# Attention and a convolutional layer on one core: fourteen of sixteen partial sums sent by transfers, four more half groups multiplied in parts

## The chip, the cores and the metric

The kernel runs on one core of one Trainium2 chip. Its time is the device time in microseconds (us). Where several runs of a kernel are shown, the median stands for them. A core has five engines that the text speaks of by short names: PE (TensorE, the matrix engine; PEld is its loading of weights), DVE (VectorE), ACT (ScalarE), POOL (GpSimd) and SP (SyncE, which here only issues transfers).

## The reference

Two layers are computed one after the other on a tensor of 4 images of 64 x 64 pixels with 256 channels. The first is self-attention over all 4096 pixels of an image. The second is a small convolutional network with a 3 x 3 local attention behind it.

```python
# layer 0, for each image: N = 4096 tokens, C = 256
q, k, v = x @ Wq + bq, x @ Wk + bk, x @ Wv + bv        # q, k: 32 channels; v: 256
attn  = softmax(q @ k.T)                               # 4096 x 4096
x     = gamma * (attn @ v) + x
# layer 1
p     = depthwise_conv3x3(x, w_perc)                   # 256 -> 768 channels
hid   = gelu(w_up1 @ p)                                # 768 -> 512
h     = x + w_up2 @ hid                                # 512 -> 256
ql, kl, vl = split(h @ w_qkv.T)                        # 256 each
w     = softmax over the 9 neighbours of (ql . kl[neighbour]) / 16
out   = h + sum over the 9 neighbours of w * vl[neighbour]
```

All tensors are in fp32.

## The kernel before

**Slots and points.** The four images are cut into 8 blocks of 512 queries each, so there are 32 slots. The kernel handles one slot after the other, and inside a slot it walks over the 4096 keys in 16 steps, called points. A point deals with one half group, which is two key tiles of 128 keys; half groups are numbered n = 0 to 15, and n = 2G + half. For a half group, PE computes the energies (`energy`, L404), ACT takes their exponentials into a tile `p` of 128 x 1024 numbers (L409), and PE multiplies the exponentials by the values into `acc` (`product`, L435, L446, L458). Energies and exponentials run two points ahead of the product that uses them: at point i the kernel issues the energy of half group i + 2, makes the pieces of half group i + 1, and issues the product of half group i.

**Three kinds of product.** A plain fp32 half group is two tiles of fp32 matmuls (L435). A half group "in parts" replaces each fp32 matmul by three cheaper fp32r matmuls. For it the exponentials are split into a high part (`ph`, made on ACT at L414), a low part (`pl`, on DVE at L502) and a gap (`pg`, on DVE at L506), and the values into matching pieces that lie in DRAM (`packed_h`, `packed_f`) and are loaded as `v` and `vf`. Half groups 2, 4, ..., 14 are in parts (`IN_PARTS`). In half groups 3, 5, ..., 13 only the second of the two tiles is in parts (`ONE_IN_PARTS`); its pieces are `oh` (ACT, L420), `ol` and `og` (DVE, L486 and L489) and the loaded `vo` (from `packed_o`). Half groups 0, 1 and 15 are plain. This holds in the 25 slots that `full(s)` names, which are slots 3 to 6, 8 to 14, 16 to 22 and 24 to 30; the remaining slots use fewer pieces.

**The softmax denominator.** It is the sum of all exponentials of a slot. Eleven of the half groups of a full slot (3, 5, 7, 9, 11, 13 and 4, 6, 8, 10, 12) are summed by transfers: POOL issues a DMA that adds `p` into one of two tiles `sent` (`send`, L476 and L478). The others (0, 1, 2, 14 and 15) are added into `den` by DVE in `add_up` (L504). At the slot's end DVE adds the two `sent` tiles to `den` (L513), folds its halves together (L514), and reduces them to `parts` (L532, L533). PE multiplies those by a fixed matrix (`dps`, L551), DVE takes the reciprocal (L554), and `on_all` spreads it over the tile by a copy (L540, DVE) and a transpose (L543). Two ACT instructions (L561) and DVE instructions (L567 to L575) then finish the block.

**What else lies in a slot.** Layer 1 runs behind attention, cut into jobs, one list entry for each point: `hidden_part` (`hid` matmuls, L779, with DVE additions at L786 and an ACT copy of `hid_a` at L792), `local_product`, `update`, `guide`, `local_values` (`lv`, L999), `scores`, `local_sum` (POOL, L1088) and `border`. At `update`, `border_terms` computes the products of border pixels on DVE, as pairs of L971 and L972: two pairs in most slots, and four in those that touch the upper or lower edge of an image. The depthwise convolution, called perceive, is 54 steps of DVE work in each slot: taps (L666) and additions of tiles (L672). A list named `share` says how many of the 54 are issued at each point, behind the point's `add_up`.

**Order.** Each engine executes its instructions in the order in which the program issues them; the order above is written out by hand in the loop over slots and points. Tiles come from pools of a fixed number of buffers. Those that matter here are `p` (3 buffers), `vs` (4 buffers, for `vo`, `oh`, `ol`, `og` and the pieces of values in the projections), `hid` (1), `xc` (2) and `sent` (1). A tile of a pool that is full waits until the oldest one is no longer used. The core of one point of the loop is:

```python
if one_in_parts(slot, point + 1): load_one(slot, point + 1)    # SP: vo
...                                                            # SP: keys, values
if in_parts(*behind): high_part(*behind)                       # ACT: ph
if one_in_parts(slot, point + 1): high_one(slot, point + 1)    # ACT: oh
if after[0] < NSLOT: energy(*after, half)                      # PE, ACT
if by_dma(slot, point + 1): send(slot, point + 1)              # POOL
...                                                            # SP: vf
for do in jobs[point]: do()                                    # layer 1
product(slot, G, half)                                         # PE
add_up(slot, *divmod(point + 1, 2))      # DVE: ol, og, pl, den, pg
... # perceive, up to sum(share[: point + 1]) steps            # DVE
```

At the first and the last point there are exceptions, which the functions below show. Between images (the last slot of each image but the fourth) the projections of the next image are issued too; `project_v` makes the pieces of the values and writes them to DRAM.

## Time and profile before

| what | value |
|---|---|
| median of three runs | 3248.18 us (3248.05 to 3251.35) |
| the profiled execution's own time | 3249.86 us |
| its span in the trace | 3248.1 us |
| granted TensorE clock, mean | 0.999 |
| POOL's transfers into `sent` | 287 of 512 KB, median 6.2 us from issue to landing |
| SP's loads of `vo` | 150 of 256 KB, median 4.1 us |
| DMA traffic | 616.58 MB, 190 GB/s on average |
| share of 16 DMA engines | 40.5% for SP's queue, 24.8% for POOL's |
| chain of waits, by engine | PE 75%, DVE 17%, issue 3%, DMA 2%, ACT 1%, POOL 1% |

The span is what the hardware profiler recorded from the first to the last instruction of one execution, and that execution's own time is 1.8 us longer. A busy share is the time in which an engine had an instruction under way, divided by the span. Line numbers such as L502 are lines of the kernel before. A name such as `pl` in a row of the profile stands for all tiles of that name.

### The profile page before, as it was taken

Reading aid. Unit: us, or ns where it says so; the run is one execution under the profiler, and the core shown is the slowest. Engines: PE = TensorE matmul, PEld = TensorE weight load, DVE = VectorE, ACT = ScalarE, POOL = GpSimd, SP = SyncE. Lnnn points to the kernel's source line nnn. Section 1 sums busy time; section 2 is a strip of 40 time slices with the busy share of each in tenths; the row PEclk is TensorE's granted clock in tenths of the full one; section 3 lists DMA queues with packets and bytes.
Section 4 is the critical chain, followed back from the end, with each engine's and each line's share of the span. In section 5 each row is a group of like instructions: output and inputs, shape, how many; then the busy total and the mean of one; then the engine's idle time right before and its main releaser. Section 6 shows DMA issues by size and latency. Waiting matters only on the chain.

```text
span 3248.1 us, 37927 instructions
## 1 busy us (share of the span) xinstructions
PE 3218.2 (99%) x12286; PEld 2223.2 (68%) x12286; DVE 2866.3 (88%) x4380; ACT 1449.8 (45%) x1845; POOL 724.1 (22%) x970
## 2 busy tenths in 40 slices
PE   9999999999999999999999999999999999999998
PEld 5557767766776677676767767776677677667655
DVE  4779899898999999988999999998799999999895
ACT  4434444444444444444444444444444444444331
POOL 3201122221222221222122222211221122222021
PEclk9999999999999999999999999999999999999999
DMA  7767766777667777667766677776777666777100
GB/s 254 222 165 202 194 187 191 202 230 205 196 187 200 211 211 191 186 196 243 205 191 193 184 200 213 208 194 192 253 210 195 190 191 185 201 210 204 49 25 28
DMA packets 289964, 616.58 MB, mean 190 GB/s; under 512 B 97424, under 2 KB 98464, under 8 KB 289632
## 3 DMA queue, kind: packets, MB, share of 16 engines
q1 hardware_dynamic: 228608, 409.47, 40.5%
q0 software_dynamic: 53472, 191.17, 24.8%
q10 hardware_dynamic: 7680, 13.44, 1.1%
q8 instruction: 102, 1.67, 0.2%
q14 instruction: 102, 0.84, 0.1%
HBM read 386.24 MB, written 76.41 MB: 142 GB/s over the span
## 4 chain that ended last, share of the span: by engine, by line
PE 75%; DVE 17%; issue 3%; DMA 2%; ACT 1%; POOL 1%; SPq 0%; ACTq 0%; DVEq 0%; POOLq 0%
PE acc L435 19%; PE acc L458 11%; PE dx L836 5%; PE e L404 5%; DVE perc L666 5%; PE hid_bc L779 5%; PE hid_de L779 4%; PE hid_gf L779 4%; PE acc L446 4%; PE v L339 3%; PE lv L999 3%; PE g L932 3%; PE lo L1133 2%; PE hid_a L779 2%; DVE den L513 2%
## 5 line engine op out<-in xcount | busy, mean ns | idle before, releaser
L666 DVE SCALAR_TENSOR_TENSOR perc<-xp,wb,perc 128x526 f32<-128x526 f32 (+1 forms) x1356 | 941.2, 758 | 1.5 <-ACT perc L662 1.4
L435 PE MATMUL acc<-p,v 128*128 128x512 f32 x1872 | 854.5, 592 | 0.2 <-ACT v L355 0.2
L409 ACT ACTIVATE p<-e 128x1024 f32<-128x1024 f32 x512 | 524.3, 1024 | 546.6 <-PE e L404 490.5
L435 PEld LDWEIGHTS acc<-p,v 128*128 128x128 f32 x1872 | 351.7, 190 | 341.9 <-issue 328.2
L478 POOL DMA_DIRECT2D sent<-p x235 | 201.3, 857 | 1125.6 <-ACT p L409 948.9
L404 PE MATMUL e<-qa,ka 128*128 128x512 f32 x1024 | 368.3, 440 | 2.0 <-ACT p L409 1.1
L414 ACT ACTIVATE ph<-p 128x1024 fp32r<-128x1024 f32 x203 | 214.3, 1056 | 213.2 <-PE acc L458 131.6
L506 DVE SCALAR_TENSOR_TENSOR pg<-pl,ph 128x1024 fp32r<-128x1024 f32 x203 | 267.2, 1316 | 9.0 <-PE e L404 0.5
L502 DVE TENSOR_TENSOR pl<-p,ph 128x1024 fp32r<-128x1024 f32 x203 | 252.2, 1242 | 18.5 <-ACT ph L414 16.8
L458 PE MATMUL acc<-ph,v 128*128 128x512 f32 x812 | 264.0, 447 | 0.2 <-DMA v<-packed_h 0.2
L404 PEld LDWEIGHTS e<-qa,ka 128*128 128x128 f32 x1024 | 189.5, 189 | 88.2 <-issue 45.7
L420 ACT ACTIVATE oh<-p 128x512 fp32r<-128x512 f32 x150 | 94.5, 630 | 317.6 <-PE acc L446 265.4
L836 PE MATMUL dx<-hid,wup 128*128 128x512 f32 x512 | 229.8, 592 | 0.0
L458 PE MATMUL acc<-pl,vf 128*128 128x512 f32 x812 | 223.3, 397 | 0.0
L458 PE MATMUL acc<-pg,vf 128*128 128x512 f32 x812 | 218.7, 391 | 0.9 <-DVE pg L506 0.9
L504 DVE TENSOR_TENSOR den<-den,p 128x1024 f32<-128x1024 f32 x161 | 207.1, 1287 | 5.7 <-ACT p L409 5.3
L1088 POOL TENSOR_TENSOR lsum<-lsum,lp 128x99 f32<-128x99 f32 (+1 forms) x179 | 208.8, 1173 | 11.7
L458 PEld LDWEIGHTS acc<-ph,v 128*128 128x128 f32 x812 | 148.2, 189 | 51.3 <-issue 26.8
L458 PEld LDWEIGHTS acc<-pl,vf 128*128 128x128 f32 x812 | 152.7, 188 | 37.1
L458 PEld LDWEIGHTS acc<-pg,vf 128*128 128x128 f32 x812 | 152.5, 188 | 37.2 <-DVE pg L506 1.4
L802 ACT ACTIVATE hid<-hid,bup 128x512 f32<-128x512 f32 x120 | 80.2, 715 | 211.0 <-DVE hid L786 211.0
L672 DVE TENSOR_TENSOR perc<-perc 128x262 f32<-128x262 f32 x360 | 167.6, 486 | 6.3
(217 smaller groups left out, 4953.3 us busy)
## 6 DMA issues: line engine op xcount, KB each, us to landing
sent<-p POOLq DMA_DIRECT2D x287, 512.0 KB, 6.2
vf<-packed_f SPq DMA_DIRECT2D x203, 512.0 KB, 5.4
v<-packed_h SPq DMA_DIRECT2D x200, 512.0 KB, 4.4
ka<-packed SPq DMA_DIRECT2D x1016, 64.0 KB, 2.8
vo<-packed_o SPq DMA_DIRECT2D x150, 256.0 KB, 4.1
xp<-in_x SPq DMA_DIRECT2D x30, 528.0 KB, 6.1
packed_f<-vlg POOLq DMA_DIRECT2D x28, 512.0 KB, 4.5
xc<-in_x SPq DMA_DIRECT2D x56, 256.0 KB, 3.9
```

Of the source, the lines that this page charges most:

```text
L404: nc.tensor.matmul(e[:, i, :], lhsT=keys[s, G][:, bass.ts(2 * half + i, P)].bitcast(F32R), rhs=queries[s].bitcast(F32R), start=True, stop= ...
L409: nc.scalar.activation(p, e, AF.Exp)
L414: nc.scalar.activation(high.bitcast(F32R), weights[s, G, half], AF.Identity, scale=BELOW)
L435: nc.tensor.matmul(accs[s][c], lhsT=v[:, i, bass.ts(c, P)], rhs=p[:, i, :], start=(first and i == 0), stop=(last and i == 1),)
L458: nc.tensor.matmul(accs[s][to + c], lhsT=w[:, i, bass.ts(c, P)].bitcast(F32R), rhs=x[:, i, :].bitcast(F32R), start=(to > 0 and n == 0 and ...
L502: nc.vector.tensor_tensor(low.bitcast(F32R), p, high, ALU.subtract)
L504: nc.vector.tensor_tensor(den, before, p, ALU.add)
L506: nc.vector.scalar_tensor_tensor(gap.bitcast(F32R), low, -SPLIT, high, ALU.mult, ALU.add)
L666: nc.vector.scalar_tensor_tensor(acc, win, wt, acc, ALU.mult, ALU.add)
L779: nc.tensor.matmul(ps[:, n * C : (n + 1) * C], lhsT=w(j), rhs=rows_of(mixes[s, j][:, kind, :]), start=(j == 0), stop=(j == MULT - 1),)
L836: nc.tensor.matmul(ps, lhsT=wup2[:, d, bass.ts(c, P)], rhs=hids[s][:, d, :], start=(d == 0), stop=(d == NHC - 1),)
L1088: nc.gpsimd.tensor_tensor(to, to, near_ws[block, half][:, t_, of, :], ALU.add)
```

## The change

Seven things change.

- Half groups 1 and 15 join those of which one tile is in parts.
- In half groups 11 and 13 the first tile is in parts as well, so that both tiles are (`BOTH_IN_PARTS`). The four pieces of the first tile lie in one buffer of the pool `hid`.
- `by_dma` of a full slot now holds for half groups 0 to 13, or 2 to 13 in the first block of an image. So DVE adds up only 14 and 15 (and 0 and 1 there). The first half group to be added is no longer known ahead, and `add_up` keeps it in `firsts` until a second one comes.
- The copy in `on_all` moves from DVE to ACT.
- The first product of each border pair (L971) moves from DVE to ACT.
- The list `share` moves perceive steps to earlier points.
- `project_v` makes and stores the additional pieces of the values, and `packed_o` has a place for two tiles of each half group. `product` is written as one list of matmuls, which lets the second accumulator start at half group 1 and end at 15.

Its core as a diff:

```diff
-ONE_IN_PARTS = (3, 5, 7, 9, 11, 13)
-BY_DMA = (ONE_IN_PARTS, (4, 6, 8, 10, 12))
+ONE_IN_PARTS = (1, 3, 5, 7, 9, 11, 13, 15)
+BOTH_IN_PARTS = (11, 13)
+BY_DMA = (3, 5, 7, 9, 11, 13)
+BY_DMA_IF_FULL = tuple(range(14))
...
+        def alone(s, n):
+            return [i for i, ns in enumerate((BOTH_IN_PARTS, ONE_IN_PARTS)) if full(s) and n in ns]
...
+        def load_alone(s, n):
+            for i in alone(s, n):
+                if i:
+                    f, *rest = [tile_of([P, NB], "vs", f"vo_{s}_{n}", 4)] + [None] * 3
+                else:
+                    four = tile_of([P, NHC, NB], "hid", f"vo_{s}_{n}_0")
+                    f, *rest = (four[:, j] for j in range(NHC))
+                forms[s, n, i], rests[s, n, i] = f, rest
+                nc.sync.dma_start(
+                    out=f.rearrange("p (f c) -> p f c", c=C), in_=packed_o[:, block(s, n // 2), i]
+                )
...
+        def high_alone(s, n):
+            for i in alone(s, n):
+                high = rests[s, n, i][0]
+                if high is None:
+                    high = tile_of([P, NB], "vs", f"oh_{s}_{n}", 4)
+                p = weights[s, n // 2, n % 2][:, i, :]
+                nc.scalar.activation(high.bitcast(F32R), p, AF.Identity, scale=BELOW)
+                highs[s, n, i] = high
...
+        def low_and_gap(s, n):
+            for i in alone(s, n):
...
+                nc.vector.tensor_tensor(low.bitcast(F32R), p, high, ALU.subtract)
+                nc.vector.scalar_tensor_tensor(
+                    gap.bitcast(F32R), low, -SPLIT, high, ALU.mult, ALU.add
+                )
...
         def product(s, G, half):
...
+                apart = alone(s, n)
+                todo += [(v[:, i], 0, p[:, i, :], F32) for i in range(2) if i not in apart]
+                for i in apart:
...
+                    todo += [
+                        (v[:, i], 0, highs[at], F32R), (f[:, :C], 0, lows[at], F32R),
+                        (f[:, C:], CH, gaps[at], F32R),
+                    ]
...
         def by_dma(s, n):
-            if n in BY_DMA[1]:
-                return full(s)
-            return 0 < s < NSLOT - 1 and (s < 2 or s % NBLK < NBLK - 1) and n in BY_DMA[0]
+            if full(s):
+                return n in BY_DMA_IF_FULL and (n > 1 or s % NBLK > 0)
+            return 0 < s < NSLOT - 1 and (s < 2 or s % NBLK < NBLK - 1) and n in BY_DMA
...
         def add_up(s, G, half):
...
-            if G == 0 and half == 0:
-                sums[s] = tile_of([P, 2, NB], "den", f"den_{s}")
-                return
...
             if not by_dma(s, n):
-                nc.vector.tensor_tensor(den, before, p, ALU.add)
+                if s in sums:
+                    nc.vector.tensor_tensor(sums[s], sums[s], p, ALU.add)
+                elif s in firsts:
+                    sums[s] = tile_of([P, 2, NB], "den", f"den_{s}")
+                    nc.vector.tensor_tensor(sums[s], firsts.pop(s), p, ALU.add)
+                else:
+                    firsts[s] = p
...
         def on_all(values, turned, out):
-            nc.vector.tensor_copy(
+            nc.scalar.copy(
                 squares(turned), values.unsqueeze(2).to_broadcast([P, NJ, SQ])
             )
...
             for to, of in border_parts(s):
-                nc.vector.tensor_scalar(edge[:, to], of(0), wc[:, 0:1], None, ALU.mult)
+                nc.scalar.mul(edge[:, to], of(0), wc[:, 0:1])
...
-            share = [1, 5, 8, 6, 5, 2, 7, 4, 6, 3, 4, 2, 1, 0, 0, 0]
+            share = [2, 6, 8, 4, 7, 2, 7, 4, 6, 4, 3, 1, 0, 0, 0, 0]
...
+                load_alone(slot, point + 1)
...
+                high_alone(slot, point + 1)
...
-                if by_dma(slot, point + 1):
-                    send(slot, point + 1)
+                at = behind[0], 2 * behind[1] + behind[2]
+                if by_dma(*at):
+                    send(*at)
```

More of the change, by code (lines that the diff above doesn't have):

```diff
@@ L204, in seen @@
             return watched[:, i : i + 1]
-        queries, keys, values, forms, staged = {}, {}, {}, {}, {}
+        queries, keys, values, forms, rests, staged = {}, {}, {}, {}, {}, {}
         packed = tc.dram_tile([NSLOT // 2, 2, 2, 2, CQK, NB], F32, name="packed")
@@ L214, in unshifted @@
         packed_f = tc.dram_tile([P, NSLOT, 2, 2 * C], F32, name="packed_f")
-        packed_o = tc.dram_tile([P, NSLOT, 2, C], F32, name="packed_o")
+        packed_o = tc.dram_tile([P, NSLOT, 2, 2, C], F32, name="packed_o")
         def in_two_sums(s):
@@ L224, in in_parts @@
             return in_two_sums(s) and 2 * G + half in IN_PARTS
-        def one_in_parts(s, n):
-            return full(s) and n in ONE_IN_PARTS
+        def alone(s, n):
+            return [i for i, ns in enumerate((BOTH_IN_PARTS, ONE_IN_PARTS)) if full(s) and n in ns]
         def load_parts(to, s, which):
@@ L322, in load_forms @@
             )
-        def load_one(s, n):
-            forms[s, n] = tile_of([P, NB], "vs", f"vo_{s}_{n}", 4)
-            nc.sync.dma_start(
-                out=forms[s, n].rearrange("p (f c) -> p f c", c=C),
-                in_=packed_o[:, block(s, n // 2)],
-            )
+        def load_alone(s, n):
[9 more added lines that the diff above has]
+                )
         def fresh(name):
@@ L345, in project_v @@
             n = 2 * (s % NBLK) + pair
-            split, one = n in IN_PARTS, n in ONE_IN_PARTS
+            split, one, both = (n in ns for ns in (IN_PARTS, ONE_IN_PARTS, BOTH_IN_PARTS))
             h = packed_h[:, s, bass.ts(pair, 2 * C)].rearrange("p (t c) -> p t c", c=C)
@@ L359, in project_v @@
                 )
-                if not split:
+                if not split and not both:
                     tiles = slice(0, 1 if one else 2)
                     nc.gpsimd.dma_start(out=h[:, tiles], in_=v[:, tiles])
+            if not split and not one:
+                return
+            high = fresh(f"vh_{s}_{pair}")
             if split:
-                high = fresh(f"vh_{s}_{pair}")
-                both = tile_of([P, 2, NB], "sent", f"vlg_{s}_{pair}")
-                both = both.rearrange("p f (t c) -> p f t c", c=C)
+                lg = tile_of([P, 2, NB], "sent", f"vlg_{s}_{pair}")
+                lg = lg.rearrange("p f (t c) -> p f t c", c=C)
+                low, gap = lg[:, 0], lg[:, 1]
                 to = h, packed_f[:, s].rearrange("p f (t c) -> p f t c", c=C)
-            elif one:
-                high = fresh(f"vh_{s}_{pair}")[:, 0:1]
-                both = fresh(f"vlg_{s}_{pair}").rearrange("p f (t c) -> p f t c", c=C)
-                of = of[:, 1:2]
-                to = h[:, 1:2], packed_o[:, s].rearrange("p f (t c) -> p f t c", c=C)
-            else:
-                return
-            low, gap = both[:, 0], both[:, 1]
+            elif both:
+                lg = tile_of([P, 2, NB], "sent", f"vlg_{s}_{pair}")
+                lg = lg.rearrange("p t (f c) -> p t f c", c=C)
+                low, gap = lg[:, :, 0], lg[:, :, 1]
+                to = h, packed_o[:, s]
+            else:
+                high, of = high[:, 0:1], of[:, 1:2]
+                lg = fresh(f"vlg_{s}_{pair}")
+                low, gap = lg[:, 0:1], lg[:, 1:2]
+                to = h[:, 1:2], packed_o[:, s, 1]
             nc.scalar.copy(low, of)
@@ L380, in project_v @@
             nc.vector.tensor_scalar(low, low, SPLIT, None, ALU.mult)
-            for at, part in zip(to, (high, both)):
+            for at, part in zip(to, (high, lg)):
                 nc.gpsimd.dma_start(out=at, in_=part)
@@ L391, in spread_queries @@
             load_parts(queries[s], s, 0)
-        weights, highs, lows, gaps, sent = {}, {}, {}, {}, {}
+        weights, highs, lows, gaps, sent, firsts, started = {}, {}, {}, {}, {}, {}, {}
         sums, accs, lsums, lrdens = {}, {}, {}, {}
@@ L415, in high_part @@
             highs[s, G, half] = high
-        def high_one(s, n):
-            high = tile_of([P, NB], "vs", f"oh_{s}_{n}", 4)
-            p = weights[s, n // 2, n % 2]
-            nc.scalar.activation(high.bitcast(F32R), p[:, 1, :], AF.Identity, scale=BELOW)
-            highs[s, n] = high
+        def high_alone(s, n):
[6 more added lines that the diff above has]
+                highs[s, n, i] = high
@@ new lines, in low_and_gap @@
+        def low_and_gap(s, n):
+            for i in alone(s, n):
+                high, (_, low, gap) = highs[s, n, i], rests.pop((s, n, i))
+                if low is None:
+                    low, gap = (tile_of([P, NB], "vs", f"o{x}_{s}_{n}", 4) for x in "lg")
+                p = weights[s, n // 2, n % 2][:, i, :]
+                nc.vector.tensor_tensor(low.bitcast(F32R), p, high, ALU.subtract)
+                nc.vector.scalar_tensor_tensor(
+                    gap.bitcast(F32R), low, -SPLIT, high, ALU.mult, ALU.add
+                )
+                lows[s, n, i], gaps[s, n, i] = low, gap
@@ L423, in product @@
         def product(s, G, half):
             p = weights[s, G, half]
-            first = G == 0 and half == 0
-            if first:
-                n = 2 * CH if in_two_sums(s) else CH
-                accs[s] = [bank("acc", f"acc_{s}_{c}") for c in range(n)]
+            n = 2 * G + half
+            if n == 0:
+                accs[s] = [bank("acc", f"acc_{s}_{c}") for c in range(2 * CH if in_two_sums(s) else CH)]
+                started[s] = set()
             v = values[s, G][:, 2 * half : 2 * half + 2]
-            last = G == NG - 1 and half == 1
@@ L431, in product @@
-            if not in_parts(s, G, half):
-                one = one_in_parts(s, 2 * G + half)
-                for i in range(1 if one else 2):
-                    for c in range(CH):
-                        nc.tensor.matmul(
-                            accs[s][c], lhsT=v[:, i, bass.ts(c, P)], rhs=p[:, i, :],
-                            start=(first and i == 0), stop=(last and i == 1),
-                        )
-                if one:
-                    at = s, 2 * G + half
-                    f = forms.pop(at)
-                    for w, to, x in (
-                        (v[:, 1], 0, highs[at]), (f[:, :C], 0, lows[at]), (f[:, C:], CH, gaps[at])
-                    ):
-                        for c in range(CH):
-                            nc.tensor.matmul(
-                                accs[s][to + c], lhsT=w[:, bass.ts(c, P)].bitcast(F32R),
-                                rhs=x.bitcast(F32R), start=False, stop=False,
-                            )
-                return
@@ L451, in product @@
-            f = forms.pop((s, G, half))
-            n = IN_PARTS.index(2 * G + half)
-            for part, (w, to, x) in enumerate((
-                (v, 0, highs[s, G, half]), (f[:, :2], 0, lows[s, G, half]), (f[:, 2:], CH, gaps[s, G, half])
-            )):
-                for i in range(2):
-                    for c in range(CH):
-                        nc.tensor.matmul(
-                            accs[s][to + c], lhsT=w[:, i, bass.ts(c, P)].bitcast(F32R),
-                            rhs=x[:, i, :].bitcast(F32R),
-                            start=(to > 0 and n == 0 and i == 0),
-                            stop=(to > 0 and n == len(IN_PARTS) - 1 and i == 1),
-                        )
+            todo = []
@@ new lines, in product @@
+            if in_parts(s, G, half):
+                f = forms.pop((s, G, half))
+                for w, to, x in (
+                    (v, 0, highs[s, G, half]), (f[:, :2], 0, lows[s, G, half]),
+                    (f[:, 2:], CH, gaps[s, G, half]),
+                ):
+                    todo += [(w[:, i], to, x[:, i, :], F32R) for i in range(2)]
+            else:
+                apart = alone(s, n)
+                todo += [(v[:, i], 0, p[:, i, :], F32) for i in range(2) if i not in apart]
+                for i in apart:
+                    at = s, n, i
+                    f = forms.pop(at)
+                    todo += [
+                        (v[:, i], 0, highs[at], F32R), (f[:, :C], 0, lows[at], F32R),
+                        (f[:, C:], CH, gaps[at], F32R),
+                    ]
@@ new lines, in product @@
+            ends = {0: n == 2 * NG - 1, CH: n == (2 * NG - 1 if full(s) else IN_PARTS[-1])}
+            for k, (w, to, x, kind) in enumerate(todo):
+                last = ends[to] and all(later[1] != to for later in todo[k + 1 :])
+                for c in range(CH):
+                    nc.tensor.matmul(
+                        accs[s][to + c], lhsT=w[:, bass.ts(c, P)].bitcast(kind), rhs=x.bitcast(kind),
+                        start=to not in started[s], stop=last,
+                    )
+                started[s].add(to)
@@ L472, in send @@
             even = 1 - n % 2
-            if n == BY_DMA[even][0]:
+            if (s, even) not in sent:
                 tag, bufs = ("xc", 2) if even else ("sent", 1)
@@ L482, in add_up @@
             n = 2 * G + half
-            if one_in_parts(s, n):
-                low, gap = (tile_of([P, NB], "vs", f"o{x}_{s}_{n}", 4) for x in "lg")
-                high = highs[s, n]
-                nc.vector.tensor_tensor(
-                    low.bitcast(F32R), weights[s, G, half][:, 1, :], high, ALU.subtract
-                )
-                nc.vector.scalar_tensor_tensor(
-                    gap.bitcast(F32R), low, -SPLIT, high, ALU.mult, ALU.add
-                )
-                lows[s, n], gaps[s, n] = low, gap
-            p = weights[s, G, half]
-            if G == 0 and half == 0:
-                sums[s] = tile_of([P, 2, NB], "den", f"den_{s}")
-                return
-            den = sums[s]
-            before = weights[s, 0, 0] if (G, half) == (0, 1) else den
+            low_and_gap(s, n)
+            p = weights[s, G, half]
             if in_parts(s, G, half):
@@ L503, in add_up @@
             if not by_dma(s, n):
-                nc.vector.tensor_tensor(den, before, p, ALU.add)
+                if s in sums:
[3 more added lines that the diff above has]
+                    nc.vector.tensor_tensor(sums[s], firsts.pop(s), p, ALU.add)
+                else:
+                    firsts[s] = p
             if in_parts(s, G, half):
@@ L510, in add_up @@
             if G == NG - 1 and half == 1:
+                den = sums[s]
                 for even in range(2):
@@ L1248, in unshifted @@
                 after = slot + (G + 1) // NG, (G + 1) % NG
-                if one_in_parts(slot, point + 1):
-                    load_one(slot, point + 1)
+                load_alone(slot, point + 1)
                 if half == 0:
@@ L1261, in unshifted @@
                     high_part(*behind)
-                if one_in_parts(slot, point + 1):
-                    high_one(slot, point + 1)
+                high_alone(slot, point + 1)
                 if after[0] < NSLOT:
                     energy(*after, half)
-                if by_dma(slot, point + 1):
-                    send(slot, point + 1)
+                at = behind[0], 2 * behind[1] + behind[2]
+                if by_dma(*at):
+                    send(*at)
                 soon = slot + (point + 3) // points, *divmod((point + 3) % points, 2)
```

## The prediction

> **What bounds the kernel now.** I read the shares of the page first, then busy time slot by slot (a slot is one block of 512 queries, cut at its `dps` matmul), then the chain of waits and the vector engine's own waits inside slots. The page's first line points at TensorE:

> ```profile
> PE 3218.2 (99%) x12286; PEld 2223.2 (68%) x12286; DVE 2866.3 (88%) x4380; ACT 1449.8 (45%) x1845; POOL 724.1 (22%) x970
> ```

> That line alone would make every matmul saved a gain. The slots say otherwise. Columns: stretch, its length, busy us of PE, PEld, DVE, ACT, POOL, PE clock, DMA share, GB/s. First slot 10, then slot 13:

> ```profile
> 933.50:1028.70 95.20, 94.35 (x369) 67.06 (x369) 88.53 (x134) 44.13 (x54) 21.57 (x25) 1.00 0.71 196
> ...
> 1312.80:1407.30 94.50, 94.25 (x369) 67.04 (x369) 87.74 (x130) 44.09 (x54) 21.95 (x24) 1.00 0.73 200
> ```

> Same matmuls, but slot 10 is 0.7 us longer, as its DVE work is 0.8 us longer (four edge pairs at L971/L972 instead of two). So DVE already sets the length of such slots. Where does DVE rest? Its waits in slot 13, complete:

> ```profile
> DVE hid L786 <- PE hid_de L779: 2.8, 1, 2.8
> DVE hid L786 <- PE hid_gf L779: 1.4, 1, 1.4
> DVE inverse L554 <- PE dps L551: 1.0, 2, 0.5
> DVE hid L786 <- PE hid_bc L779: 0.4, 1, 0.4
> ```

> All lie in points 15 to 2 of the sixteen points. From the `hid_bc` add of point 2 (1336.29) to the last `parts` (1407.15), 70.9 us, DVE has no listed wait, and PE needs `parts` for `dps`, the last matmul of the slot. The loop is therefore: 23.5 us of PE from `dps` to that `hid_bc`, then 70.9 us of DVE. PE keeps pace beside it, and in the slots with two edge pairs the chain ends through both (start, length, what):

> ```profile
> 1368.21 1.72 PE acc L435 x4
> 1369.93 1.40 PE acc L446 x6
> ...
> 1394.27 1.07 ACT ph L414
> ...
> 1395.37 1.23 DVE pl L502
> ...
> 1407.29 0.41 PE dps L551 x2
> ```

> `ph` of half group 14 waits for PE's product 12; from the `pl` behind it the tail is fixed DVE work of 11.8 us to `parts`, while PE has as much left. The two arrive in a tie.

> [...] 99% busy hides that 22 of 32 `dps` wait for DVE or start 0.2 us late. [...] (start, length):

> ```profile
> 1014.56 1.27 POOL L1065 TENSOR_TENSOR lp<-lp,near 128x396 f32<-128x396 f32 x1 [2.79 <-ACT lp L1060]
> ...
> 1015.04 1.34 DVE L489 SCALAR_TENSOR_TENSOR og<-ol,oh 128x512 fp32r<-128x512 f32 x1
> ```

> That `og` took 1.34 us instead of 0.69. [...] ACT at 45% has room. [...] GpSimd's transfers and Sync's share the 16 engines; q1 (40.5%) and q0 (24.8%) do here.

> **The change, part by part** (25 "full" slots; other slots keep their product matmuls).

> *PE.* A half group in plain fp32 is eight records, 3.43 us in the chain; one key tile in parts is 1.72 + 1.40 = 3.12; both in parts 2 x 1.40 = 2.80. Half groups 1 and 15 save 0.31 each, 11 and 13 0.32 each: 1.26 us a slot, 31.5 us in all. Only half group 1 lies ahead of the `hid_bc` of point 2; the rest runs beside the DVE chain.

> *DVE, prices by start-to-start distance in slot 13:* `ol`+`og` 1.32 (1392.71 to 1394.03), `den` add of 14 1.34, a tap of `perc` 0.68, an L971 0.25, a copy at L540 0.45. Whole slot: 4 pairs +5.28, 3 adds -4.02 at most, 2 copies -0.90, 2 L971 -0.50: about nothing. But place counts. Ahead of the `hid_bc` of point 2, where DVE rests 4.6 us, lie the pair of half group 1, the adds of 1 and 2 and both copies: none of that moves the end. Behind it:
> - pairs of 11, 13, 15: +3.96
> - add of 14 gone: -1.34; but `pg` 14 now follows `pl` at once, and such neighbours are 1.25 instead of 1.14 apart: +0.11
> - new `share`: 8 taps by the end of point 1 instead of 6: -1.36
> - two L971 gone: -0.50

> Sum +0.87; the start is 0.31 earlier: **+0.55 us a slot**, for the 15 with two edge pairs. For the 7 with four, two more L971 go: +0.05. In slots 8, 16, 24 (first of an image) half groups 0 and 1 aren't sent, so 14 and 15 are both added as before: +0.55 + 1.34 = +1.9. Total 8.3 + 0.4 + 5.7 = 14.4 us. Bounds a slot: below, -0.6 if the 1.34 us of the last L672 in slot 13 (0.42 alone), which covered the wait for `ph`, shrinks as `ph` comes 0.6 earlier; above, +0.4 for `og`/`ol` 15 standing in POOL's 7.6 us of L1088, where the adds took 0.1 to 0.3 longer.

> *ACT.* Four `oh` more (0.63 each), the copies and L971s: about 4.5 us a slot on an engine that idles 50. One place is near the path: at the slot's end the copy now waits for the reciprocal (done 0.8 after `dps`) with two L561 (1.05), `oh` of 1 (0.63), the exponential (0.92) and the L792 copy of `hid_a` (0.37) queued behind it. With 0.6 for the copy (nearest row: `vlg` L376, 586 ns) L792 ends 4.4 after `dps`; PE's `lv` reuses that bank and starts at 4.7. Cost: 0 taken, 0 to +0.4 as bounds. DVE's transpose waits about 0.2 longer there and has the rest to cover it.

> *DMA, POOL, SP.* 69 more transfers of 512 KB, mostly at points 15 to 1, where the DMA share is 0.26 to 0.5; POOL issues each in 0.6 to 0.9 and idles 78%. The ring buffer `p` is freed by landing (median 6.2 us) against the two points (over 10 us) that it has. 100 loads of 256 KB on SP, two of a slot's four at points 10 and 12. Loads of 13 wait for product 11, as the `vo` load there already did; behind them SP holds keys and `v`. Share there is about 1. Cost 0 taken, since PE gains slack; above, see the third case.

> *Elsewhere.* Projections split four more pairs per image, and the last blocks' copies on ACT lie in an exposed chain (5 local reciprocals, at 0.2 each): +1.

> Sum: 14.4 + 1 = +15 against the profiled execution's 3249.9 (span 3248.1 and 1.8 around it); the median of runs is 1.7 lower, so 3248.2 + 15 = **3263 us**.

> **Rivals.**
> 1. *DVE grows behind point 2* (above): slower, 3263. For it: no DVE wait in 70.9 us, and slot 10 against 13. Chance 0.6 that it shows.
> 2. *The tail starts with PE*: faster. If DVE reaches `pl` 14 no later than `ph` 14 is ready, the slot follows PE's product 12, which comes 0.31 + 0.32 earlier, with a tail longer by 0.1: -0.5 for 15 slots; slots with four edge pairs lose their 0.7 too, -1.2 for 7; +0.8 for 3: -14, so 3234. It decides from 0.6 us less DVE work than I count. For it: the tie at 1395.37. Against: it needs POOL's masks to hit less. PE's whole 31.5 (3217) is shut out by the tail. Chance 0.2.
> 3. *Sums cancel*: half of the bounds each way, near 3248. Chance 0.15.
> 4. *Loads late*: 0.8 MB more at points 10 to 14, at some 270 GB/s 3 us; `v` of product 14 is issued at 1015.09, lands in 4.5, is used at 1020.89: slack 1.3, so 1.7 of wait, of which PE's lead at the end covers most. With 0.5 left in 22 slots and case 1: 3274. Chance 0.05.
> That the change doesn't do what it says is out: the built program has 200 fp32 matmuls less, 600 in parts more, 69 adds less.

> **How the numbers follow.** Runs of this kernel can tell 0.2% (6.5 us) from no change. Faster is case 2: 0.20. Within 0.2% is case 3 and the near edge of case 1: 0.20. Slower is the rest of 1, and 4: 0.60. Range: low 3238, leaving out the far end of case 2; high 3284, case 1 with its upper bounds (0.4 in 25 slots = 10, ACT's 0.4 = 10).

> **What would show it.** Right: PE busy about 93 of 95 us in slot 13, with 2 us before `dps` ended by DVE `parts`; DVE without waits from point 2 on; slots 8, 16, 24 grown most, slot 10 hardly. DVE busy near 88.5, ACT near 49. Wrong: full slots below 94.2 us, `pl` waiting for `ph` 14 (case 2); PE waiting for `v` or `vo` (case 4); or DVE resting behind point 2.

## The result, and the profile after

| | before | after |
|---|---|---|
| median of runs | 3248.2 us | 3338.0 us (3334.1 to 3357.6) |
| ratio to before | 1 | 1.0286, 95% interval 1.0245 to 1.0327 |
| profiled execution, span | 3249.9, 3248.1 us | 3334.1, 3332.4 us |
| granted clock, mean | 0.999 | 0.988 |

A few executions in the series below fell into a slower state; all medians and ratios are of the others. The change makes the kernel 90 us slower, where 15 were predicted. The page's first line after:

```profile
PE 3218.1 (97%) x12486; PEld 2281.4 (68%) x12486; DVE 2892.0 (87%) x4391; ACT 1570.1 (47%) x2105; POOL 745.5 (22%) x1047
```

TensorE is busy exactly as long as before (3218), although some 31 us of matmul time were taken out. That is the first hint: something made its matmuls slower, and the granted clock says so (0.988, and 0.999 before). Cutting both traces at their `dps` matmuls tells where the added 84.3 us of span lie:

| part | before | after | difference |
|---|---|---|---|
| slot 0 | 113.6 | 126.5 | +12.8 |
| slots 7, 15, 23 (projections of the next image) | 396.6 | 419.2 | +22.5 |
| the 25 full slots | 2364.3 | 2409.3 | +45.0 |
| behind the last `dps` | 112.7 | 116.6 | +3.9 |

Slots 1, 2 and 31 are within 0.1 us of before. Most of the last row is not the change's: of the kernels profiled below that run the same code there, some show 113.9 to 114.1 and the others 116.7 to 117.7, so at most 1.2 us of it can be.

A slot has here the number of the `dps` that ends it. Slot 10 was shown of before; the stretch that the prediction calls slot 13 (1312.80 to 1407.30) is slot 14 by this count. Slot 13 took 94.4 us before and has two edge pairs like slot 14. Now slots 10, 13 and 29 (columns as before: length, busy PE, PEld, DVE, ACT, POOL, PE clock, DMA share, GB/s):

```profile
962.80:1058.60 95.80, 93.27 (x377) 68.58 (x377) 88.84 (x133) 48.53 (x64) 23.47 (x29) 1.00 0.82 221
1254.60:1351.60 97.00, 94.51 (x376) 69.83 (x376) 88.74 (x131) 48.06 (x62) 22.52 (x28) 0.98 0.82 222
2891.00:2986.40 95.40, 92.87 (x377) 68.64 (x377) 88.54 (x131) 48.05 (x62) 22.48 (x28) 1.00 0.84 230
```

Slots 13 and 29 do the same work. Slot 29 has it done in 95.4 us with TensorE busy for 92.9; slot 13 needs 97.0, TensorE is busy for 94.5, and its clock is 0.98. TensorE's timeline at the start of slot 13 (start, length, what, and in brackets the idle time before) shows why:

```profile
1251.41 0.62 PE L480 MATMUL acc<-og,vo 128*128 128x512 f32 x2
1254.60 0.59 PE L565 MATMUL dps<-parts,fold 128*128 128x32 f32 x2 [2.58 <-DVE parts L547]
1255.01 1.20 PE L417 MATMUL e<-qa,ka 128*128 128x512 f32 x2
1256.01 2.49 PE L793 MATMUL hid_a<-perc,wup 128*128 128x256 f32 x6
1258.34 1.46 PE L793 MATMUL hid_bc<-perc,wup 128*128 128x256 f32 x6
```

TensorE pauses for 2.58 us until DVE has `parts`. Behind the pause six `hid_a` matmuls take 2.49 us, and the next six of the same kind 1.46. The same place in stretches gives the clock as the last figure but two:

```profile
1252.03:1254.60 2.57, 0.00 (x0) 0.00 (x0) 2.38 (x4) 0.00 (x0) 0.00 (x0) 1.00 0.87 289
1254.60:1258.20 3.60, 3.60 (x10) 2.97 (x11) 2.24 (x4) 2.57 (x5) 0.50 (x2) 0.53 0.97 336
1258.20:1262.00 3.80, 3.80 (x19) 3.33 (x18) 3.55 (x8) 3.10 (x5) 0.63 (x2) 1.00 0.18 70
```

So the clock fell to about half (0.53 in a stretch of 3.60 us) for some 3.4 us. In slot 7 ACT's timeline shows another pause, and what ended it:

```profile
744.68 0.58 ACT L389 COPY vlg<-v 128x512 f32<-128x512 f32 x1 [2.26 <-DMA packed_f<-vlg]
...
752.87 0.59 ACT L389 COPY vlg<-v 128x512 f32<-128x512 f32 x1 [5.25 <-DMA packed_o<-vlg]
```

The copy of one pair of value tiles waits for the transfer of the pair before to land. Both write `vlg`, and `project_v` takes it from the pool `sent`, which has one buffer. Before, the pairs of half groups 11 and 13 had `vlg` in `vs`. TensorE waits behind that copy, at L997, for 4.05 us.

Last, the end of slot 14 in the chain of waits (start, length, what):

```profile
1434.66 2.28 PE acc L480 x10
...
1437.02 0.64 ACT oh L436
...
1437.72 0.87 DVE ol L445
...
1439.50 1.40 DVE den L515
...
1440.93 1.24 DVE den L527
...
1447.06 0.30 PE dps L565
```

The tail starts at TensorE's product of half group 13. `oh` of 15 comes from `vs`, whose four buffers hold the pieces of 13 until then. Behind `oh` stand `ol`, `og`, all den additions, the transposes and the reductions, 10.1 us to `dps`. Beside this TensorE has only the rest of product 13, two energies and products 14 and 15. Ahead of `dps` the chain also names a transfer of `xc`; the two transfers of `xc` there landed at 1447.94 and 1448.84, after `dps` had begun, and `parts` ended at 1447.01, so it is `parts` that `dps` waited for.

The chain is not the only bound there. These are all of DVE's waits from the `hid_bc` addition of point 2 (1374.84) to `dps` in the same slot (us in total, times, longest):

```profile
DVE hid L800 <- PE hid_bc L793: 0.4, 1, 0.4
DVE lo L1160 <- PE lo L1147: 0.2, 1, 0.2
```

The first wait is the one ahead of that addition. Behind it DVE rests for 0.2 us in 72, and it is busy until `ol` of 15 begins. So DVE's own work ends as late as the chain through `oh`.

### The profile page after: what moved, and what is told of

It is laid out like the page before. It is cut to its first block, busy times and chain, and to the rows that moved or that the text cites. A ratio compares the mean times of both kernels' runs of the same rounds, so it can differ in the third digit from the quotient of the medians.

```text
span 3332.4 us, 39180 instructions
## 1 busy us (share of the span) xinstructions
PE 3218.1 (97%) x12486; PEld 2281.4 (68%) x12486; DVE 2892.0 (87%) x4391; ACT 1570.1 (47%) x2105; POOL 745.5 (22%) x1047
## 4 chain that ended last, share of the span: by engine, by line
PE 76%; DVE 13%; issue 4%; DMA 3%; POOL 2%; ACT 1%; SPq 1%; ACTq 0%; DVEq 0%; POOLq 0%
PE acc L480 35%; PE dx L850 6%; PE e L417 6%; PE hid_de L793 5%; PE hid_gf L793 5%; PE hid_bc L793 5%; PE lv L1013 3%; DVE perc L680 3%; PE lo L1147 3%; PE hid_a L793 2%; PE v L347 2%; PE g L946 2%; DVE den L527 1%; PE s L1054 1%; DVE pl L509 1%
## 5 line engine op out<-in xcount | busy, mean ns | idle before, releaser
L480 PE MATMUL acc<-p,v 128*128 128x512 f32 x1472 | 679.1, 596 | 0.2 <-ACT v L363 0.2
L499 POOL DMA_DIRECT2D sent<-p x304 | 257.7, 848 | 1497.0 <-ACT p L422 951.9
L480 PEld LDWEIGHTS acc<-p,v 128*128 128x128 f32 x1472 | 278.5, 191 | 270.6 <-issue 258.6
L519 DVE SCALAR_TENSOR_TENSOR pg<-pl,ph 128x1024 fp32r<-128x1024 f32 x203 | 250.6, 1235 | 11.2
L436 ACT ACTIVATE oh<-p 128x512 fp32r<-128x512 f32 x200 | 126.5, 633 | 253.2 <-issue 79.1
L480 PEld LDWEIGHTS acc<-ph,v 128*128 128x128 f32 x812 | 149.7, 191 | 51.9 <-issue 26.8
L480 PE MATMUL acc<-oh,v 128*128 128x512 f32 x400 | 184.8, 543 | 0.0
L1102 POOL TENSOR_TENSOR lsum<-lsum,lp 128x99 f32<-128x99 f32 (+1 forms) x179 | 163.7, 921 | 11.7
```

Of the source, the lines that this page charges most:

```text
L480: nc.tensor.matmul(accs[s][to + c], lhsT=w[:, bass.ts(c, P)].bitcast(kind), rhs=x.bitcast(kind), start=to not in started[s], stop=last,)
L499: nc.gpsimd.dma_start(out=sent[s, even], in_=p, accum_op=ALU.add)
L519: nc.vector.scalar_tensor_tensor(gap.bitcast(F32R), low, -SPLIT, high, ALU.mult, ALU.add)
L1102: nc.gpsimd.tensor_tensor(to, to, near_ws[block, half][:, t_, of, :], ALU.add)
```

## The experiments

They fall into four groups: two cures, the share, the tail, and the parts alone. "Full slots" are given for two edge pairs, without half clock behind their pause, unless said otherwise.

**The buffer of the pieces of values.**

```diff
             elif both:
-                lg = tile_of([P, 2, NB], "sent", f"vlg_{s}_{pair}")
...
+                low, gap = (fresh(f"v{x}_{s}_{pair}") for x in "lg")
+                to = h, packed_o[:, s, :, 0], packed_o[:, s, :, 1]
```

> Edit: in the projections, the low parts and gaps of the values of half groups 11 and 13 go into two buffers of the pool vs instead of the single buffer of the pool sent; all else as in the changed kernel. Theory (the single buffer makes consecutive pairs wait for each other's transfers): slot 0 loses its pauses of 4.1 and 3.7 us and the half clock behind them, 12.9 us; slots 7, 15 and 23 lose pauses of 3.7 to 4.5 us and the half clock behind them, 22.5 us; together about 35 us, so 3303 us. Rival (the scalar engine's added work in those slots delays the projections): no change, 3338 us.

Measured: 3305.4 us (ratio to before 1.0176, 1.0158 to 1.0195). Slot 0 takes 113.9 us (113.6 before), and slots 7, 15 and 23 take 400.8 instead of 419.2. The theory holds: 33 us came from one buffer that consecutive pairs share. (The edit also stores the two pieces by two transfers instead of one, which was not tested apart.)

**Matmuls of ones in the pause.**

```diff
-            ps = bank("m", f"dps_{s}")[:, :n]
+            ps = bank("m", f"dps_{s}")
+            for _ in range(10 if full(s) else 0):
+                nc.tensor.matmul(ps[:, :P], lhsT=ones, rhs=ones, start=True, stop=True)
+            ps = ps[:, :n]
```

> Edit: ten matmuls of 128x128 ones (about 2.3 us at full clock) in front of dps in the 25 full slots, into the bank that dps overwrites, where TensorE pauses 2.2 to 3.7 us in the changed kernel. Theory (a pause of more than some 2 us lets the granted clock fall to a half for the 3.4 or 6.8 us behind it): no half clock at slot ends, full slots 95.4 us (two edge pairs) and 95.75 (four), 20 us less, 3318 us. Rival one (the half clock has another cause, such as load or transfers): half clock stays, 3338 us. Rival two (the added matmuls delay dps): 3340 us or more.

Measured: 3314.5 us (1.0199, 1.0177 to 1.0221), 23.5 less than with the change alone. TensorE's timeline and the stretch behind `dps` of slot 12:

```profile
1243.66 2.39 PE L565 MATMUL dps<-ones 128*128 128x128 f32 x20
1246.41 0.41 PE L568 MATMUL dps<-parts,fold 128*128 128x32 f32 x2 [0.35 <-DVE parts L547]
...
1247.20 1.46 PE L796 MATMUL hid_a<-perc,wup 128*128 128x256 f32 x6
```

```profile
1246.41:1250.00 3.59, 3.59 (x17) 3.16 (x18) 2.42 (x6) 2.75 (x5) 0.50 (x2) 1.00 0.89 280
```

`dps` comes no earlier within its slot, yet the six `hid_a` take 1.46 us instead of 2.49. Useless work on TensorE makes the kernel faster, so here it is the pause itself that lowers the clock: 0.53 behind it in the changed kernel, 1.00 with the matmuls of ones. The DMA share in that stretch is 0.89, nearly as high as the 0.97 of the stretch at half clock, so the transfers are not the cause.

**Both cures together.** The two edits above in one kernel.

> Edit: the buffers vs for the pieces of the values, and ten matmuls of ones in front of dps in full slots, together. If the three causes add up (projections' waits 33 us, half clock 22 us, the rest DVE's longer work): 3338 - 33 - 22 = 3283 us, with full slots at 95.4 (two edge pairs) and 95.75 us (four). If the half clock would come back in other places: 3300 us.

Measured: 3281.3 us (1.0101, 1.0085 to 1.0118). The causes add up: beside the kernel with the buffers alone, the matmuls of ones take off 24.1 us. Of the time over before 33 us remain: the full slots now sum to 2391.1 us, 26.8 over before, most of them at 95.4 to 95.5 us with two edge pairs and 95.75 with four.

**The share alone, and with the buffers.**

```diff
-            share = [2, 6, 8, 4, 7, 2, 7, 4, 6, 4, 3, 1, 0, 0, 0, 0]
+            share = [5, 7, 4, 4, 7, 2, 7, 4, 6, 4, 3, 1, 0, 0, 0, 0]
```

> Edit: share = [5, 7, 4, 4, 7, 2, 7, 4, 6, 4, 3, 1, 0, 0, 0, 0], so 12 perceive steps instead of 8 lie ahead of the hid_bc of point 2. Theory (the full slots are set by DVE's work behind point 2): 4 taps of 0.68 us move into DVE's rests at points 0 and 1; the pause before dps shrinks from 2.5 us to under 0.7, the half clock behind it goes, full slots about 93.3 us (TensorE busy there 92.9), which is 80 us less in 25 slots: 3259 us. Rival (the rests at points 0 and 1 are too short or lie in the wrong place, and the taps push hid additions and PE back by as much): full slots stay above 95, 3330 us.

> The edits of the buffers for the pieces of the values (vs instead of sent) and of share together. If both theories hold and the two sums add up: 3338 - 35 - 79 = 3224 us, faster than the kernel before (3248). If the gain of share is only the half clock that goes (20 us): 3283 us.

Measured: 3339.4 us (1.0269, 1.0251 to 1.0288), and with the buffers 3310.8 (1.0189, 1.0132 to 1.0246). Both miss: full slots stay at 95.4 us with pauses of 2.5. Four taps more ahead of point 2 bring nothing.

**The share of before**, with both cures, so that little half clock blurs it.

> Edit: as with both cures (vs buffers and matmuls of ones), but with the list share of the kernel before, which puts 6 instead of 8 steps ahead of point 2 and the same 20 up to point 3. If the stretch of DVE without rest begins at the hid_bc of point 2, as the prediction had it, full slots grow by 1.36 us: 30 us more than the kernel with both cures and the new share, some 3313 us. If it begins at the hid_gf of point 3: no change against that kernel, 3283 us.

Measured: 3316.8 us (1.0205, 1.0188 to 1.0222), 35.5 more than with the new share; slot 14 takes 96.7 us against 95.5. (In the profiled execution pauses of 1.5 to 1.9 us were left behind most of the matmuls of ones, and half clock followed six of them; in slot 14 there is none.) So in the other direction the share does count, by 1.3 us a slot. DVE's work behind point 2 was a real bound, and in the changed kernel it ends level with another one, which hides a further gain.

**Half groups 11 and 13 with one tile in parts as before** (`BOTH_IN_PARTS = ()`).

> Edit: BOTH_IN_PARTS = () in the changed kernel, so half groups 11 and 13 have one tile in parts as before; 1 and 15 stay, as do the fourteen sums by transfers, the copies and first border products on the scalar engine and the new share. Theory (the two added pairs of DVE work, 2.64 us a slot, stand in the stretch that sets the slot's end, and with them go the pauses, the half clock behind them and the projections' waits for the buffer sent): full slots set by TensorE, 92.9 + 0.64 = 93.5 to 93.9 us, slot 0 and slots 7, 15, 23 as before, in all 3230 us, faster than the kernel before. Rival (the sums by transfers or the work on the scalar engine cost the time): 3300 us or more.

Measured: 3287.4 us (1.0116, 1.0099 to 1.0133). It misses, and it is the run that named the other bound. Slot 13 of this kernel:

```profile
1228.49:1324.21 95.72, 93.62 (x373) 67.83 (x373) 84.30 (x127) 46.72 (x60) 20.22 (x28) 1.00 0.83 218
```

DVE is busy for over 4 us less than in the changed kernel (3.4 of them for the four instructions that went), and the slot is no shorter than the 95.4 us there. What this kernel gains lies in slot 0 and slots 7, 15 and 23 (36 us in the trace), since the pieces of 11 and 13 no longer go through `sent`, and in less half clock. Now DVE waits where it did not before. Its longest waits in slot 22:

```profile
DVE pl L509 <- ACT ph L427: 2.2, 1, 2.2
DVE ol L445 <- ACT oh L436: 2.2, 2, 2.0
```

The chain at the same slot's end shows no other engine in between:

```profile
2215.52 2.66 PE acc L480 x8
...
2218.25 0.64 ACT oh L436
...
2218.92 0.92 DVE ol L445
...
2220.47 1.23 DVE den L515
...
2227.87 0.30 PE dps L565
```

**Half group 15 in plain fp32 as well** (`ONE_IN_PARTS` ends at 13).

> Edit: as without both tiles of 11 and 13, and half group 15 in plain fp32 too. Theory: DVE has 1.32 us a slot less in its last stretch, TensorE 0.31 more. If TensorE sets full slots by then, they are 0.3 longer than with 15 in parts: 3237 us. If DVE still sets them, they are up to 1.3 us shorter: 3215 us.

Measured: 3232.8 us, 0.9952 of before (0.9936 to 0.9969): faster than both kernels, between the two expected values. In its slots TensorE has no pause:

```profile
1303.94:1397.63 93.69, 93.69 (x371) 67.54 (x370) 83.68 (x125) 46.02 (x59) 21.81 (x26) 1.00 0.82 215
```

**The tail cut in two ways.** In the first, `ol` and `og` of 15 are made behind the den additions; this was run with the `vs` buffers for the values, then also with the longer share, and then with `BOTH_IN_PARTS = ()`.

```diff
-            low_and_gap(s, n)
+            if n < 2 * NG - 1:
+                low_and_gap(s, n)
...
                         nc.vector.tensor_tensor(den, den, sent.pop((s, even)), ALU.add)
+                low_and_gap(s, n)
```

> Edit: with the pieces of the values in vs, and in the last half group the low part and gap of 15 are made on DVE after the den additions instead of ahead of them. New theory: two chains end together in the changed kernel's full slots, DVE's work from point 2 on, and a tail of 10.1 us from TensorE's product 13 (whose oh buffer oh 15 takes over) through oh, ol, og, four den additions, transposes and reductions to dps, beside which TensorE has only 7.5 us of work. Moving ol and og of 15 behind the additions cuts the tail alone: DVE's sum stays, so full slots stay at 95.4 us and the time at 3300 us (kernel with vs buffers alone: 3305). If the tail alone were the bound: full slots 93.5 us, 3255 us.

> Edit: the pieces of the values in vs, ol and og of 15 behind the den additions, and the share with 12 steps ahead of point 2, together. New theory (both chains have to be cut at once; the share alone brought nothing since the tail held, and the late pieces alone bring nothing since DVE's sum holds): no pause before dps over 1 us, no half clock, full slots 93.0 to 93.5 us, 3235 us, faster than the kernel before. Rival (a third chain, such as the hid additions of point 3 that wait for TensorE): full slots above 94.5 us, 3265 us or more.

> Edit: BOTH_IN_PARTS = () and ol and og of 15 behind the den additions. In the kernel without both tiles of 11 and 13, DVE had 2.64 us a slot less to do and full slots stayed at 95.5 to 95.9 with a pause of 2.1 us. New theory (the tail behind product 13 held them): with the tail cut, TensorE sets full slots at 93.5 us, 3228 us, which is 59 us less than without this edit. Rival (something else holds the end): no change, 3287 us.

In the second, the pieces of 15 lie in `hid`, again with `BOTH_IN_PARTS = ()`.

```diff
-                if i:
+                if i and n < 2 * NG - 1:
```

> Edit: BOTH_IN_PARTS = (), and the four pieces of half group 15 lie in the pool hid instead of vs, so oh 15 no longer waits for product 13 to leave its buffer. The order on DVE stays as in the changed kernel. New theory: oh 15 starts with its exponential, 1.5 us earlier, and the tail ends 1.5 us earlier: full slots 94.2 us, 3250 us. If the wait for the buffer is not what starts the tail: no change, 3287 us.

Measured: late pieces 3291.0 us (1.0126, 1.0109 to 1.0143), full slots 95.2; with the share 3292.8 (1.0141, 1.0124 to 1.0158), full slots 95.2; late pieces without both tiles of 11 and 13 3252.3 (1.0013, 1.0006 to 1.002), full slots 94.2 to 94.3; pieces in `hid` 3256.9 (1.0025, 1.0012 to 1.0037), full slots 94.35 to 94.45. Four of these kernels make a square of full slots:

| | tail as in the change | `ol`, `og` of 15 late |
|---|---|---|
| 11 and 13 with both tiles in parts (`vs` buffers) | 95.4 | 95.2 |
| 11 and 13 with one tile in parts | 95.5 to 95.9 | 94.2 to 94.3 |

Each cut alone brings 0.2 us or nothing, both together 1.1 to 1.2. Two bounds that lie level explain this: DVE's sum of work and the tail. The square is not quite clean: with one tile in parts products 11 and 13 take TensorE longer, so product 13 leaves its buffers later (86.05 us behind the slot's start in slot 22, 85.30 in slot 14 of the changed kernel) and the tail with it, which is how 95.5 to 95.9 can exceed 95.4. The pieces in `hid` leave DVE's order alone and cure only the wait of `oh`, and they give the same. So the wait for the buffer is what starts the tail.

The share on top of the late pieces missed its 93.5 us. In slot 12 of that kernel DVE's list of waits ends, but for 0.4 us at `lo`, with the `hid` additions of point 3:

```profile
DVE hid L800 <- PE hid_gf L793: 2.9, 2, 1.4
DVE hid L800 <- PE hid_de L793: 1.0, 2, 0.8
```

Each of the two waits occurs twice, at points 1 and 3. The taps that moved ahead of point 2 only made room for a new rest at point 3; behind it DVE works on to `parts`. That is read from the trace and wasn't tested on its own.

**Both cuts of the tail in one kernel**, with `BOTH_IN_PARTS = ()`.

> Edit: BOTH_IN_PARTS = (), ol and og of 15 behind the den additions, and the pieces of 15 in the pool hid. Theory: each of the two cuts of the tail alone gave full slots of 94.3 and 94.4 us; together TensorE sets them at 93.5 us (its busy time), 3230 us, no slower than the version with 15 in plain fp32 (3233). Rival (a further bound at 94.3): 3250 us.

Measured: 3252.6 us (1.0015, 1.0008 to 1.0021), full slots 94.25 to 94.3, a miss. The chain of slot 13 now starts elsewhere:

```profile
1298.23 0.95 PE acc L480 x4
...
1299.25 1.07 ACT ph L427
...
1300.35 1.24 DVE pl L510
...
1312.32 0.41 PE dps L567 x2
```

It is the tail that the prediction's second rival named, from product 12 over `ph` 14. A pair of 15 anywhere behind `ph` 14 lengthens it.

**Half group 15 alone, on the kernel before**: 15 is added to `ONE_IN_PARTS`, and the stop flags of its matmuls follow.

> Edit: the kernel before, with half group 15 added to those with one tile in parts and nothing else changed. Theory (the tail: oh 15 waits for product 13 to leave its buffer, and ol, og and the den additions behind it take 10 us to dps, while TensorE has some 7 us of work): pauses of 1.9 to 2.4 us before dps, now and then half clock behind them, full slots 95.8 to 97 us instead of 94.5, 3285 to 3310 us. Rival (half group 15 is cheap, since TensorE saves 0.31 us a slot and DVE has one pair more, 1.32): 3248 + 25 x 1.3 = 3281 us at most, no half clock.

Measured: 3315.4 us (1.0209, 1.0192 to 1.0226), worse than the top of what was expected. Full slots take 96.2 to 96.7 us, or 97.7 to 98.4 where half clock lies behind their pause of 2.3 to 2.6 us. This single edit, which saves TensorE 0.31 us a slot, costs 67 us. Not all of this is the wait for the buffer. In slot 13 DVE's only listed wait behind the `hid_bc` addition of point 2 is this:

```profile
DVE ol L487 <- ACT oh L420: 0.5, 1, 0.5
```

So of the 1.8 us that the slot grows, `oh` 15 accounts for 0.5 and the added DVE work for the rest; in slot 11, with four edge pairs, DVE does not wait for `oh` at all, and the slot grows by 1.5. In all the full slots take 59 us more, half clock included.

**The changed kernel without 15** (with the `vs` buffers).

> Edit: the changed kernel with the pieces of the values in vs and half group 15 in plain fp32; 11 and 13 stay with both tiles in parts. Theory: DVE's sum from point 2 on is 1.32 us less and the tail behind product 13 is gone: full slots 94.1 (two edge pairs) to 94.4 us (four), pauses before dps under 1.2 us, no half clock, 3248 us. If 15 plays no part: 3305 us, as with vs buffers alone.

Measured: 3252.1 us (1.0008, 0.9999 to 1.0017): full slots 93.9 to 94.3, one 94.6, as expected. This edit takes away the tail and a pair of DVE work at once, so it does not tell the two apart; the square does.

**The scalar engine's new work undone** in the fast version.

```diff
-            nc.scalar.copy(
+            nc.vector.tensor_copy(
...
-                nc.scalar.mul(edge[:, to], of(0), wc[:, 0:1])
+                nc.vector.tensor_scalar(edge[:, to], of(0), wc[:, 0:1], None, ALU.mult)
```

> Edit: the version without both tiles of 11 and 13 and with 15 in plain fp32 (3233 us), with the copies of on_all and the first border products back on DVE. Theory (TensorE sets its full slots at 93.7 us and DVE has rests): no change, 3233 us. If the moves to the scalar engine carry its gain: 0.5 us more in 18 slots and 1.0 in 7, 3249 us.

Measured: 3230.4 us (0.9948, 0.9931 to 0.9965). The interval overlaps that of the fast version: the moves bring nothing there. Which of the other parts (half group 1 in parts, fourteen sums by transfers, the share) make the fast version some 15 us faster than before was not tested.

## Why the prediction was right or wrong

**Direction right, size wrong by a factor of six.** Of the added 90 us some 33 are the projections' buffer, some 23 the half clock, and with both cured 33 remain, where 15 were forecast. So two steps failed: the term "Elsewhere, +1", and the pause before `dps`, which was foreseen and stood in the sum with nothing. The sum for the full slots had the right bound and came out too small.

**The term "Elsewhere, +1" was 35 us** (12.8 in slot 0 and 22.5 in three slots). It counted four more split pairs and not where their pieces lie. `both` takes `vlg` from `sent`, and half groups 10 to 14 then use that one buffer in a row. With other buffers 33 us went.

**The step "2 us before `dps`" was seen and not priced.** The prediction listed this pause as a sign that it was right. The pause came, 2.1 to 3.7 us in all full slots but one, and its cost did not stop at its end: the clock behind it was not in the sum. Half clock followed 73 of the 185 pauses of 1.9 to 2.9 us in the last section.

**What bounds the full slots: right, but too small.** The signs that were named came: in slot 14 DVE has next to no rest from point 2 on, in slot 29 TensorE is busy for 92.9 of 95.4 us and DVE for 88.5, and with both cures slots 8, 16 and 24 grew most. In slot 30 DVE's stretch takes 72.2 us (from 3009.58 to the end of `parts` at 3081.77) instead of 70.95 (2930.49 to 3001.44), so +1.25 where the sum said +0.87. The difference has the size of the upper bound named there, and the instructions that it spoke of did take longer: `ol` and `og` of 15 stand in POOL's L1102 (6.25 us from 3068.31 on) and take 0.86 and 0.96 us instead of 0.69, and a gap of 13 took 1.34. That they are the whole difference is not shown. The start came 0.33 earlier (0.31 forecast). The share's credit of 1.36 measured 1.3. Full slots without half clock grew by 0.9 to 1.1 us with two edge pairs (0.55 forecast), by 0.5 to 0.6 with four (0.05), and by 2.4 in slots 8 and 16 of the kernel with both cures (1.9), so by 0.3 to 0.6 us more than forecast in each kind.

**A second bound that the prediction did not have.** It counted the pair of 15 as a mere 1.32 us of DVE time. The tail was worked out for `ph` of 14 behind product 12, and the pieces of 15 were not followed to their own start: `vs` has four buffers, the pieces of 13 fill them, and `oh` of 15 has to wait for product 13. In the changed kernel this costs a slot no more than some 0.2 us, since DVE's sum ends as late; that the two lie level is chance. But it shuts out gains. Where the text hoped for them (the second rival, "from 0.6 us less DVE work than I count"), 2.64 us less by its prices brought none. The fast version's 3233 us lies beside that rival's 3234 by chance: it is another kernel, without the pair of 15, and its bound is TensorE.

**Costs taken as 0 held.** ACT's queue at the slot's end and its other new work cost nothing measurable in the fast version, and the additional sums by transfers are in that version as well. DVE's waits for the copies on ACT were longer than the 0.2 us of the text (0.7 and 1.8 us in slot 14), but they lie where DVE rested before. TensorE waiting for loads of `v` (the fourth case) shows mainly where DVE holds it up less, as in the changed kernel without 15: 0.5 to 1.2 us in 17 of its full slots.

## What to carry to other kernels

## What the runs showed of the hardware

The price of a pause was not expected. In the profiles of fifteen of these kernels, the one before and the changed one among them and those with matmuls of ones left out, TensorE's pauses of over 0.6 us behind the first 30 us were compared with the clock in the 9 us that follow:

| pause | with half clock behind it |
|---|---|
| 0.6 to 1.6 us | 1 of 182 |
| 1.6 to 1.9 us | 1 of 10 |
| 1.9 to 2.2 us | 8 of 31 |
| 2.2 to 2.9 us | 65 of 154 |
| over 2.9 us | 24 of 24 |

For nearly the same pause half clock comes in some slots and not in others. In the changed kernel TensorE pauses for 2.58 us ahead of slot 13, with half clock behind it, and for 2.52 us ahead of slot 14, without. The clock record of that trace shows a difference between the two. From 30 us to the last matmul it has 15 stretches at half clock, ten of 3.41 us and five of 6.83. Their starts and ends lie whole steps of 3.413 us apart, to within 0.005 us; the starts 1254.68 and 1783.75, for example, are 155 steps apart. Here is the step with the pause ahead of slot 13, behind which the clock is at half from 1254.68 on, and then three steps around the pause ahead of slot 14 (columns as before; the first busy time is TensorE's, the clock is the last figure but two):

```profile
1251.27:1254.68 3.41, 0.83 (x5) 0.36 (x3) 3.11 (x5) 0.00 (x0) 0.42 (x2) 1.00 0.89 307
...
1346.84:1350.25 3.41, 2.27 (x9) 1.18 (x7) 3.31 (x5) 0.23 (x1) 0.64 (x2) 1.00 1.00 381
1350.25:1353.67 3.42, 2.03 (x10) 1.81 (x11) 2.20 (x4) 1.19 (x3) 1.06 (x3) 1.00 0.91 301
1353.67:1357.08 3.41, 3.41 (x18) 2.99 (x17) 3.34 (x8) 3.41 (x6) 0.89 (x2) 1.00 0.90 353
```

The first pause, 2.58 us, lies in one step. The second, 2.52 us, is cut into 1.14 and 1.39 us by the end of a step, and the clock stays at 1.00. These are all steps at full clock in the changed kernel's trace, between 30 us and the step of the last matmul:

| TensorE's rest in one step | next step at half clock |
|---|---|
| under 1.55 us | 0 of 920 |
| 1.55 to 1.9 us | 1 of 9 |
| over 1.9 us | 14 of 14 |

What half clock costs can be read from slots with the same work. Slot 12 has 6.83 us at half clock (1155.70 to 1162.52) and takes 98.6 us, where slot 13 with 3.41 takes 97.0 and slot 29 without takes 95.4:

```profile
1155.97:1254.60 98.63, 96.06 (x376) 70.94 (x376) 88.72 (x131) 48.16 (x62) 24.01 (x29) 0.97 0.79 216
```

All this is one trace of one kernel. That a pause is hit in one execution and missed in the next would fit the scatter of the changed kernel's runs, 3334 to 3358 us, but it is not shown.
